# Two transformer blocks on one core: the first attention projects raw x in ten shared score steps

## The chip, the cores and the metric

The kernel runs on one core of a Trainium2 chip, in fp32, written in Bass with the Tile framework. The metric is the time of one execution on the device in microseconds (us). Lower is better. The engines of the core work beside each other: TensorE (PE, matmuls and transposes, with its weight loads PEld), VectorE (DVE), ScalarE (ACT), GpSimd (POOL) and SyncE (SP, which issues transfers). Line numbers such as L728 are lines of the kernel before.

## The reference

Two pre-norm blocks act on x of shape 8 x 512 x 256 (sequences, tokens, width):

```python
x = x + attention0(layernorm(x))   # 16 heads of 16, 4 k/v heads, rope, causal
x = x + moe0(layernorm(x))         # 32 experts, 8 per token, inner width 96
x = x + attention1(layernorm(x))   # 16 heads of 16, biases, causal
x = x + moe1(layernorm(x))         # 16 experts, 2 per token, inner 176, and a shared expert of 352

def attention0(x):                 # Wq 256x256, Wk and Wv 256x64, Wo 256x256
    q, k, v = rope(x @ Wq), rope(x @ Wk), x @ Wv
    att = softmax(where(causal, q k^T / sqrt(16), -inf))
    return (att @ v) @ Wo
def moe0(x):
    probs = softmax(x @ router_w.T)          # 32 logits per token
    rw, sel = top_k(probs, 8); rw = rw / sum(rw)
    return sum over chosen experts e of  rw_e * (silu(x @ wg_e) * (x @ wu_e)) @ wd_e
```

The layernorm has no scale and no shift: (x - mean) / sqrt(var + 1e-5), over the 256 features of a token.

## The kernel before

**Stages.** Attention 0 goes through the eight sequences. Beside sequence b it prepares sequence b+1 and finishes b-1: it adds the attention's output to x, normalizes, routes, and scatters each token's normalized row to 8 rows of a table in DRAM (`xg`), sorted by expert. Then the experts of layer 0 run tile by tile. Attention 1 gathers their results back to tokens, and has the same structure as attention 0. The experts of layer 1 come last.

**Score steps.** A sequence has four head groups c of four heads. Four blocks of keys j (128 keys each) are needed per group; block j meets only queries from 128j on, so it is 512, 384, 256 or 128 columns wide. `BANKS` makes three score steps of a group: block 0 (512 columns for each of four heads), blocks 1 and 3 together (512), block 2 (256). That is 12 steps per sequence. A step is: 4 or 8 matmuls into one tile `st` of four PSUM banks (L728; there is one such tile), one exponential on ACT from it to SBUF (L733; 2048 columns, or 1024 for block 2), and the causal mask by DVE on the diagonal squares (L739). The next step's scores can start when the exponential has read `st`. When a group's probabilities are masked, its 32 values products follow (L751), then a copy, four transposes to tokens (`turn`) and a division by the row sum.

**Order.** The order on PE is written by hand. `PLAN0` (attention 0) and `PLAN1` (attention 1) have one word per step; after the step's scores and exponential, each letter issues one piece of other work: c a values product, t its turn, m the mask, p a piece of `before` of the next sequence, q one of the sequence after that, a a piece of `finish` of the sequence before (output, then `after0`: normalization, routing, weights, tables), o the rest of the finish before that, g gathers. `planned` reads the words. DVE, ACT and POOL are ordered by the scheduler of the framework from priorities that follow the order of issue. `SENT` says how many of a sequence's 32 waiting scatters each step releases, 3, 3 and 2 in attention 0; a released scatter there is paced by that step's exponential.

**Preparing a sequence, attention 0** (`before`). x arrives transposed (`xf`, 256 features x 512 tokens). `load_x` turns it into tokens with 8 transposes and two ACT copies. DVE does statistics, the inverse root (L311 to L320) and the normalization (L358, 4 x 128x256). `turned` transposes the normalized x back (8 transposes L372, two ACT copies L373). Per tile of 128 tokens, two matmuls make q, k, v (384 columns, L952) and DVE does the rotations (three products L959 to L965, two sums) and a copy of v. Then q and k are transposed, with a copy each on ACT; k has two copies, each scaled by half[:,0:1] or half[:,1:2], one on ACT (L991) and one on DVE (L992).

**Finishing** (`finish`). `output` transposes the attention's output (two copies on ACT), makes two halves of the output product (8 matmuls of 256 columns each, L806) and adds each to x. `routed0` calls `layernorm` whole, in one piece of the order, then `turned`; `route` multiplies by the router (8 matmuls, L385), copies, transposes the logits (L393), and does maximum, difference, exponential (L405, ACT), the eight largest, weights, ranks within each expert (small matmuls L437, L439) and the list of scatters (L460).

## Time and profile before

| | us |
|---|---|
| median of the runs shown (1528.22, 1534.38, 1543.1) | 1534.38 |
| the profiled execution, its own time | 1529.75 |
| its span in the trace | 1528.0 |
| first exponential of attention 0 | 30.09 |
| first exponentials of its sequences 1 to 7 | 73.85, 115.80, 158.13, 201.01, 243.57, 288.90, 331.81 |
| experts 0, about | 380 to 805 |
| first exponentials of attention 1, sequences 0 to 7 | 808.28, 855.33, 906.23, 965.25, 1024.90, 1084.83, 1144.01, 1203.01 |
| experts 1, about | 1306 to 1490 |

The terms of the prediction are read from the trace as follows. The busy time of an engine is the sum of its instructions in a window. The timeline lists instructions of an engine in order: start, duration (with xN, of a run of N together), line, operation, output and inputs, partitions x columns; brackets give the idle time before the row and what ended it. The mean clock that TensorE was granted over this execution was 0.974 of full speed; where it is low, the same matmul takes longer.

### The profile page before, as it was taken

How to read it: one execution, taken by the hardware profiler on the slowest of the kernel's cores; microseconds unless marked ns; L12 is line 12 of the kernel's file. 1: busy time of each engine (PE TensorE's matmuls, PEld its weight loads, DVE VectorE, ACT ScalarE, POOL GpSimd, SP SyncE). 2: the span in 40 equal slices, each digit the busy share in tenths (PEclk: the TensorE clock that was granted, in tenths of full speed). 3: DMA queues.
4: the chain of work that ended last, by engine and by line, in shares of the span. 5: the costliest groups of instructions: out<-in, count | busy, mean ns of one | idle time of the engine just before them, and what ended most of it. 6: DMA issues, size and time to landing. Idle time of an engine off the chain costs nothing.

```text
span 1528.0 us, 29822 instructions
## 1 busy us (share of the span) xinstructions
PE 1405.0 (92%) x9856; PEld 960.7 (63%) x9856; DVE 949.3 (62%) x3121; ACT 666.6 (44%) x885; POOL 811.0 (53%) x674
## 2 busy tenths in 40 slices
PE   5889998887999899999998899999999988999994
PEld 3355555444889799999884445545455454777773
DVE  4678888776575566555565567677576564544454
ACT  2566666664233223333334455646645642122222
POOL 0004777777456100388878888888884203233433
PEclk8999999999999999999998999999999999999997
DMA  2023555336999786899997556566452005353346
GB/s 73 23 70 111 171 163 163 133 137 204 269 294 295 251 258 200 221 264 269 276 263 133 70 73 142 70 144 115 83 71 72 32 24 176 96 173 114 110 159 241
DMA packets 229312, 237.22 MB, mean 155 GB/s; under 512 B 77820, under 2 KB 209281, under 8 KB 229154
## 3 DMA queue, kind: packets, MB, share of 16 engines
q1 hardware_dynamic: 172930, 145.73, 32.3%
q0 software_dynamic: 55872, 89.18, 25.6%
q8 instruction: 84, 1.38, 0.4%
q14 instruction: 74, 0.61, 0.1%
q10 hardware_dynamic: 352, 0.33, 0.1%
HBM read 125.79 MB, written 110.92 MB: 155 GB/s over the span
## 4 chain that ended last, share of the span: by engine, by line
PE 59%; DVE 13%; POOL 8%; ACT 7%; issue 7%; DMA 5%; SPq 0%; DVEq 0%; ACTq 0%; POOLq 0%
PE gu_m L1314 16%; PE y_m L1343 11%; PE st_a L728 7%; PE o_a L751 5%; POOL x_a L1423 5%; ACT p_a L733 5%; PE xgT_m L1282 5%; POOL xg L460 3%; PE hT_m L1333 3%; DVE p_a L739 3%; DMA xg<-xn_f,rows_f 3%; PE sy_f L506 2%; PE sg_f L493 2%; PE k_a L1077 1%; PE su_f L493 1%
## 5 line engine op out<-in xcount | busy, mean ns | idle before, releaser
L460 POOL DMA_INDIRECT xg<-xn_f,rows_f x320 | 324.0, 1013 | 363.2 <-ACT p_a L733 134.7
L1423 POOL DMA_INDIRECT x_a<-yg,yrows x256 | 403.8, 1577 | 204.9 <-DMA xg_m<-xg 122.8
L733 ACT ACTIVATE p_a<-st_a 128x2048 f32<-128x2048 f32 (+1 forms) x192 | 306.1, 1594 | 233.4 <-PE st_a L728 132.4
L1314 PE MATMUL gu_m<-gw,xgTs_m 128*128 x1416 | 303.3, 358 | 0.4 <-DVE xgTs_m L1284 0.4
L1314 PEld LDWEIGHTS gu_m<-gw,xgTs_m 128*128 128x128 f32 x1416 | 235.2, 192 | 25.5 <-DVE xgTs_m L1284 1.2
L728 PE MATMUL st_a<-qT_a,kT_a 32*128 32x512 f32 (+3 forms) x2048 | 199.9, 483 | 34.6 <-ACT p_a L733 27.4
L1343 PE MATMUL y_m<-dw,hTs_m 96*128 (+1 forms) x860 | 216.9, 382 | 2.9 <-issue 2.9
L739 DVE TENSOR_TENSOR p_a<-p_a,causal 128x512 f32<-128x512 f32 x256 | 170.2, 683 | 76.1 <-ACT p_a L733 74.6
L1348 ACT COPY ys_m<-y_m 128x512 f32<-128x512 f32 x177 | 103.6, 585 | 175.1 <-PE y_m L1343 158.2
L1284 DVE COPY xgTs_m<-xgT_m 128x512 f32<-128x512 f32 x177 | 121.6, 687 | 85.4 <-PE xgT_m L1282 85.1
L728 PEld LDWEIGHTS st_a<-qT_a,kT_a 32*128 32x128 f32 x2048 | 88.4, 188 | 128.0 <-ACT p_a L733 55.1
L751 PE MATMUL o_a<-p_a,v 128*32 128x512 f32 (+3 forms) x2048 | 157.9, 447 | 10.3 <-DVE p_a L739 10.3
L1343 PEld LDWEIGHTS y_m<-dw,hTs_m 96*128 96x128 f32 (+1 forms) x860 | 150.1, 191 | 16.9 <-issue 3.1
L1306 DVE SCALAR_TENSOR_TENSOR h_m<-h_m,xg_m,gu_m 128x96 f32<-128x96 f32 (+1 forms) x354 | 104.0, 325 | 83.0 <-ACT h_m L1319 38.9
L1356 POOL DMA_INDIRECT yg<-ys_m,to_m x76 | 80.0, 1053 | 126.3 <-ACT ys_m L1348 113.5
L751 PEld LDWEIGHTS o_a<-p_a,v 128*32 128x32 f32 x2048 | 57.6, 111 | 130.5 <-issue 94.5
L1334 DVE COPY hTs_m<-hT_m 96x256 f32<-96x256 f32 (+1 forms) x177 | 83.9, 474 | 74.1 <-PE hT_m L1333 74.1
L1322 ACT ACTIVATE h_m<-gu_m 128x192 f32<-128x192 f32 x139 | 45.9, 330 | 176.7 <-PE gu_m L1314 162.7
L1282 PE MATMUL xgT_m<-ident,xg_m 128*128 128x128 f32 x708 | 110.4, 278 | 11.1 <-DMA xg_m<-xg 8.6
L1282 PEld LDWEIGHTS xgT_m<-ident,xg_m 128*128 128x128 f32 x708 | 88.2, 143 | 33.0 <-issue 13.0
L1333 PE MATMUL hT_m<-ident,h_m 128*96 128x128 f32 (+1 forms) x430 | 77.2, 275 | 0.3 <-DVE h_m L1306 0.2
L806 PE MATMUL y_a<-wo,oT_a 128*128 128x256 f32 x256 | 62.3, 388 | 5.0 <-DVE x_a L511 4.8
(249 smaller groups left out, 1614.5 us busy)
## 6 DMA issues: line engine op xcount, KB each, us to landing
xg_m<-xg SPq DMA_DIRECT2D x354, 144.0 KB
yg<-ys_m SPq DMA_DIRECT2D x139, 256.0 KB
g<-yg SPq DMA_DIRECT2D x16, 512.0 KB
xg<-zeros SPq DMA_DIRECT2D x50, 144.0 KB
xg<-xn_f,rows_f POOLq DMA_INDIRECT x320
x_after<-x_in SPq DMA_DIRECT2D x8, 512.0 KB
x_a<-x_after SPq DMA_DIRECT2D x8, 512.0 KB
x_a<-yg,yrows POOLq DMA_INDIRECT x256
```

What stands on the lines that cost most here:

```text
L460: inst = nc.gpsimd.indirect_dma_start(out=lay.xg, out_offset=bass.IndirectOffsetOnAxis(ap=rows[:, t, i : i + 1], axis=0), in_=xn[:, t, :], ...
L728: nc.tensor.matmul(st[:, g, at : at + T - j * P], kT[r, j * P : (j + 1) * P], qT[r, j * P :], start=True, stop=True,)
L733: self.newest = nc.scalar.activation(pt, st[:, :, :width], AF.Exp, scale=SCALE).ins
L739: self.masked = nc.vector.tensor_tensor(d, d, causal.unsqueeze(1).to_broadcast([P, NG, P]), ALU.mult).ins
L751: nc.tensor.matmul(o[32 * g : 32 * g + 32, j * P :], v1[:, j, v_at + g * (DH + 1) :][:, :32], probs[n][:, g, at : at + T - j * P], start=( ...
L1282: nc.tensor.transpose(tr[:, j, c, :], xg[:, j, c * P : (c + 1) * P], ident)
L1284: nc.vector.tensor_copy(xT, tr)
L1306: nc.vector.scalar_tensor_tensor(h[:, j, :], h[:, j, :], xg[:, j, D:][:, bass.ds(offs[part, i + j][2], 1)], gus[j][:, inner:], ALU.mult, A ...
L1314: nc.tensor.matmul(gus[j], xT[:, j, c, :], gu[:, bass.ds(at + c * 2 * inner, 2 * inner)], start=(c == 0), stop=(c == ND - 1),)
L1333: nc.tensor.transpose(hp[:n_in, q, j, :], h[:, j, lo : lo + n_in], ident)
L1343: nc.tensor.matmul(y[:, j, :], hT[:n_in, q, j, :], dn[:n_in, bass.ds(at + q * D, D)], start=(q == 0), stop=(q == n_ch - 1),)
L1423: inst = nc.gpsimd.indirect_dma_start(out=xs[b][:, t, :], out_offset=None, in_=lay.yg[: most_rows(b, again), :], in_offset=bass.IndirectOf ...
```

## The change

1. *Ten steps.* `STEPS` replaces `BANKS`. Two head groups form a pair with five steps: (group 0: block 0), (group 0: blocks 1, 3), (both groups: block 2, 256 columns each), (group 1: block 0), (group 1: blocks 1, 3). Each has an exponential of 2048 columns. This holds in both attentions. `ready` queues a group's values product when all its blocks have been through a step: after the third step of a pair for the first group, after the fifth for the second. The order strings are new, and `SENT` is 3, 3, 4, 3, 3.
2. *Raw x is projected* (attention 0). The weights of q, k, v and the router (32 more columns, 416 in all) are centred once: the mean of each column over the 256 features is made by a matmul with a matrix of 1/256 (`even`) and subtracted. So `xf` as it comes from DRAM is the input of the q, k, v matmuls, and neither the normalized x nor its transposition is needed; statistics and inverse root still are. The root is multiplied in by the rotations, now scalar_tensor_tensor, and by the copy of v. `xf` has two buffers. ACT copies the 32 router columns into `sums`.
3. *The router in the output product* (attention 0). Once, in sequence 1's preparation, `output_routing` makes Wo times the centred router weights, as 32 more columns of Wo. The output product is 288 wide, in four tiles of 128 tokens instead of two halves; DVE adds 256 columns to x and 32 to `sums`. So `sums` holds the logits of the new x, up to the root. `route` then has no router matmuls, copy or turn: it takes the maximum of `sums`, subtracts, multiplies by the root, ends its piece of the order, and takes the exponential in the next. The last sequence, routed beside the experts, goes the same way.
4. *Routed normalization in pieces.* `routed0` gives out statistics, root and normalization in pieces of the order of PE, not whole.
5. *Both copies of k* are on ACT. Three tiles (`q_in`, `turned0`, and the weights for `output_routing`) take room in other pools.

The diff, cut to its core:

```diff
-PLAN0 = "com optpm oapaom com apom atom acm qppm tqqm cm aappm tpm"
+PLAN0 = "ocmoo otom poaaom mc taapma comapa tpm qqqm cmpp taaam"
 TAIL0 = "otoaoaoaoa"
-PLAN1 = "cooggm oggm toggm coaggm aopggm taaoggm cppaoggm ppoggm taaopggm caopm aopam tapopm"
+PLAN1 = "cooggm ootggm oaggm coaggm toapggm acoggpm taaopggm ppaoggm caopggm taopppm"
 TAIL1 = "otaaoaaaoaoaoaa"
 PB = (3, 2)
-SENT = ((3, 3, 2), (1, 1, 1))
+SENT = ((3, 3, 4, 3, 3), (1, 1, 1, 1, 1))
...
-BANKS = [[0], [1, 3], [2]]
-QOFF = {0: (0, 0), 1: (1, 0), 3: (1, 3 * P), 2: (2, 0)}
+STEPS = [(0, [0]), (0, [1, 3]), (None, [2]), (1, [0]), (1, [1, 3])]
+QOFF = {0: 0, 1: 0, 3: 3 * P, 2: 2 * P}
...
+        roots[name] = rstd
         yield
+        if tag is None:
+            return rstd
...
+            if xT is None:
+                lg = sums.pop(b)
+            else:
...
+                nc.vector.tensor_tensor(pe, pe, roots.pop(name).unsqueeze(2).to_broadcast([P, NT, n_e]), ALU.mult)
+            if xT is None:
+                yield
             nc.scalar.activation(pe, pe, AF.Exp)
...
+        def blocks(self, at):
+
+            pair, n = divmod(at, len(STEPS))
+            side, js = STEPS[n]
+            return [(2 * pair + h, j, h if side is None else 0) for h in ((0, 1) if side is None else (side,)) for j in js]
+
+        def scores(self, b, at):
+
+            name = f"a{self.n}_{b}_{at}"
             st = self.ps.tile([P, NG, T], F32, tag="st", name=f"st_{name}", bufs=1)
-            for j in js:
-                at = QOFF[j][1]
+            pt = self.ptp.tile([P, NG, T], F32, tag="p2" if at % len(STEPS) == 2 else "p01", name=f"p_{name}", bufs=1 if at % len(STEPS) == 2 else PB[self.n])
+            for c, j, h in self.blocks(at):
...
+                self.probs[c, j] = pt, lo
+            self.newest = nc.scalar.activation(pt, st, AF.Exp, scale=SCALE).ins
...
+        def ready(self, at):
+
+            pair, n = divmod(at, len(STEPS))
+            done = 2 * pair + (n >= 2) + (n >= 4)
+            while self.next_c < done:
+                self.queue.append((self.b, self.next_c, self.probs))
+                self.next_c += 1
...
+            if self.n == 0:
+                for t in range(NT):
+                    y = self.bank(f"y_{name}_{t}")[:, : D + E0]
+                    for k in range(ND):
+                        nc.tensor.matmul(
+                            y, oT[:, k, t * P : (t + 1) * P], self.wo[:, k, :], start=(k == 0), stop=(k == ND - 1)
+                        )
+                    nc.vector.tensor_tensor(x[:, t, :], x[:, t, :], y[:, :D], ALU.add)
+                    nc.vector.tensor_tensor(sums[b][:, t, :], sums[b][:, t, :], y[:, D:], ALU.add)
+                    if t % 2:
+                        yield
+                return
...
+        nc.vector.tensor_copy(wq[:, :, width - E0 :], rw[:, 0, :, :E0])
+        even = awp.tile([P, P], F32, tag="even", name="even")
+        nc.vector.memset(even, 1.0 / D)
...
+        mean = bank("mean")[:, :width]
+        for k in range(ND):
+            nc.tensor.matmul(mean, even, wq[:, k, :], start=(k == 0), stop=(k == ND - 1))
+        for k in range(ND):
+            nc.vector.tensor_tensor(wq[:, k, :], wq[:, k, :], mean, ALU.subtract)
...
+                both = bank(f"wor_{k}")[:, :E0]
+                for m in range(ND):
+                    nc.tensor.matmul(
+                        both, woT[:, m, k * P : (k + 1) * P], wq[:, m, width - E0 :], start=(m == 0), stop=(m == ND - 1)
+                    )
+                nc.scalar.copy(wo[:, k, D:], both)
...
-            x = xs[b]
-            xn = layernorm(x, lnp, name)
+            xf = kept.pop(b)
+            root = whole(layernorm_steps(xs[b], lnp, name, None))
+            sums[b] = lasting[0].tile([P, NT, E0], F32, tag="sums", name=f"sums_{b}", bufs=3)
             yield
-            xn = yield from turned(xn, lnp, bank, name)
...
+                        tok[:, :width], xf[:, k, t * P : (t + 1) * P], wq[:, k, :],
...
+                nc.scalar.copy(sums[b][:, t, :], tok[:, width - E0 : width])
+                by = root[:, t : t + 1]
+                nc.vector.scalar_tensor_tensor(
+                    a, qk, by, cos[:, t, :].unsqueeze(1).to_broadcast([P, n_h, DH]), ALU.mult, ALU.mult
+                )
...
+                nc.vector.tensor_scalar(
+                    v_heads(v1, t, NG), tok[:, n_h * DH :][:, : HKV * DH].rearrange("p (g d) -> p g d", g=HKV),
+                    by, None, ALU.mult,
...
-            nc.vector.tensor_scalar(kT[:, 1, :], tr, half[:, 1:2], None, ALU.mult)
+            nc.scalar.activation(kT[:, 1, :], tr, AF.Copy, scale=half[:, 1:2])
...
-        xf = tmp.tile([P, ND, T], F32, tag="xf", name=f"xf{b}", bufs=1)
+        xf = tmp.tile([P, ND, T], F32, tag="xf", name=f"xf{b}", bufs=2)
...
-            xn = layernorm(xs[b], lnp, name, "xn_rows", 2, E0)
-            yield
-        xT = yield from turned(xn, lnp, bank, name)
-        yield from route(0, b, xn, xT, name, False)
+            xn = yield from layernorm_steps(xs[b], lnp, name, "xn_rows", 2, E0)
+        yield from route(0, b, xn, None, name, False)
```

## The prediction

> **What bounds the kernel now.** I read the page first. Its first part names TensorE (PE).
>
> ```profile
> PE 1405.0 (92%) x9856; PEld 960.7 (63%) x9856; DVE 949.3 (62%) x3121; ACT 666.6 (44%) x885; POOL 811.0 (53%) x674
> ```
>
> Then I cut the span into stages: the first attention 28 to 375 us (its sequences start where the first exponential of each starts), experts 395 to 805, the second attention 806 to 1256, the rest. One row each, of a steady sequence, the experts, and a steady sequence of the second attention (columns: window, its length, busy time of each engine, TensorE clock, DMA share, GB/s):
>
> ```profile
> core 0: us, PE busy (x) PEld busy (x) DVE busy (x) ACT busy (x) POOL busy (x), PEclk, DMA share, GB/s
> 201.01:243.57 42.56, 38.40 (x377) 21.99 (x376) 35.04 (x132) 27.35 (x29) 33.05 (x32) 1.00 0.56 173
> 395.00:805.00 410.00, 403.68 (x2520) 366.92 (x2519) 246.34 (x732) 131.75 (x284) 214.09 (x167) 0.99 0.95 262
> 1024.90:1084.83 59.93, 58.04 (x425) 31.09 (x421) 40.10 (x131) 33.71 (x32) 49.61 (x34) 1.00 0.62 103
> ```
>
> Experts and second attention are full (98 and 97%). The first attention is not: 4.2 us in 42.6 are gaps. Its timeline on PE shows three of them in the last quarter of a sequence; brackets give the idle time before a row and its releaser.
>
> ```profile
> 231.20 1.93 PE L751 MATMUL o_a<-p_a,v 128*32 128x512 f32 x24
> 235.06 0.64 PE L751 MATMUL o_a<-p_a,v 128*32 128x256 f32 x8 [1.93 <-DVE p_a L739]
> 235.63 1.15 PE L728 MATMUL st_a<-qT_a,kT_a 32*128 32x384 f32 x16
> 236.71 1.09 PE L372 MATMUL xT_f<-ident,xn_f 128*128 128x128 f32 x8
> 237.64 0.60 PE L982 MATMUL qT_a<-ident,qr_a 128*128 128x128 f32 x4
> 239.26 0.66 PE L982 MATMUL qT_a<-ident,qr_a 128*128 128x128 f32 x4 [1.02 <-ACT xT_f L373]
> ...
> 242.36 1.14 PE L728 MATMUL st_a<-qT_a,kT_a 32*128 32x512 f32 x8 [0.78 <-ACT kT_a L991]
> ```
>
> So PE work sets the pace, plus 3.7 us in which a mask comes late on a crowded VectorE (DVE) or a copy late on ScalarE (ACT). GpSimd (POOL) is as full, since each scatter is followed by 0.30 us:
>
> ```profile
> L460 POOL DMA_INDIRECT xg<-xn_f,rows_f x32 | 33.6, 1048 | 9.7 <-issue 8.8 <-ACT xT_f L373 0.3 <-ACT xT_a L373 0.3
> ```
>
> 33.6 + 8.8 = 42.4 of 42.56 us. In sequence 5 the tables of the first experts add a wait of PE on DVE, after which PE runs at half speed for some 3 us:
>
> ```profile
> 286.30 0.34 PE L1167 MATMUL ex<-past,step 32*1 32x106 f32 x2 [1.99 <-DVE past L1164]
> 286.48 0.34 PE L1169 MATMUL ro<-past,nt 32*1 32x106 f32 x2
> 286.75 2.09 PE L728 MATMUL st_a<-qT_a,kT_a 32*128 32x512 f32 x8
> 288.77 3.02 PE L751 MATMUL o_a<-p_a,v 128*32 128x512 f32 x32
> ```
>
> **The change, per sequence of the first attention.** Costs on PE are distances from start to start in the timeline at 201 to 243 us: scores of 512 columns 1.07, of 384+128 1.08, of 256 0.64, a values product 2.29, qkv of one tile 1.33 (384 columns), a half of the output 1.83 (8 matmuls of 256), four transposes 0.5.
>
> *Removed from PE*: transposes of the normalized x (1.0) and of the router's input (1.0), the router (0.55) and its turn (0.3): 2.85. *Added*: 32 columns on qkv and output. 0.229 us a matmul at 256 columns and 0.334 at 384 give 0.82 ns a column, so 16 matmuls take 16 x 32 x 0.82 ns = 0.4. PE work falls by 2.4.
>
> *ACT* loses four copies of 0.59 and one of 0.27, and gets four of 32 columns (0.19 each, on the line through 0.27 at 128 and 0.585 at 512) and the second k copy (0.69). That copy lies beside the 1.14 us of scores that the next exponential waits for; uncovered it costs 0.69. Ten exponentials of 1.88 replace eight of 1.88 and four of 1.03.
>
> *DVE* loses the normalization (1.37) and the k copy (0.74); it gains four adds of 32 columns (0.7), a multiply by the root (0.29) and smaller adds to x (4 x 0.42 for 2 x 0.68). The rotations become scalar_tensor_tensor. Row L1306 has such a one, 0.305 us at 96 columns, where the rotations' line (0.48 at 320, 0.311 at 160) gives 0.24; row L791 shows no surplus (0.217 at 64 columns). So 0 to 0.06 each, 0 to 0.7 for twelve; I take 0, the nearest plain form.
>
> *Ten steps.* A step is its scores and then other PE work until the exponential frees the score banks: 0.07 us to its start, 1.88, 0.06 back. So a step takes at least 3.15 us (3.3 with the two 256-column blocks). By the changed kernel's order on PE, steps 0 to 9 take 3.36, 3.16, 3.75, 3.36, 7.1 (a turn, four outputs, a qkv tile), 4.8, 3.15, 3.36, 4.4, 3.75 (the last holds its exponential and then 0.69 of k copy): 40.2.
>
> *The wait that is added.* On ACT the router's exponential stands ahead of the exponential of step 6. It needs DVE, and behind it on ACT wait a copy of sums and exponential 6, for which PE's step 7 waits. DVE has to do, after the fourth output: adds and statistics (1.6), a rotation (1.55 from start to start), more statistics, maximum and difference (0.85), the root's chain, two normalizations, one mask, two normalizations and the multiply. Rows of the chain:
>
> ```profile
> 223.28 0.35 DVE L311 TENSOR_SCALAR v_f<-mv_f 128x4 f32<-128x4 f32 x1
> ...
> 225.65 0.16 DVE L320 SCALAR_TENSOR_TENSOR rstd_f<-w_f,rstd_f 128x4 f32<-128x4 f32 x1
> 226.06 1.48 DVE L358 TENSOR_SCALAR xn_f<-x_in,mv_f,rstd_f 128x256 f32<-128x256 f32 x4 [0.25 <-DMA xg<-xn_f,rows_f]
> ```
>
> The chain is 2.15 from its second link (223.66) to 225.81, then 0.25 to the next row, 0.7 for two normalizations, 0.6 a mask, 0.7, and 0.3: 1.6 + 1.55 + 0.85 + 2.15 + 0.25 + 0.7 + 0.6 + 0.7 + 0.3 = 8.7. The fourth output ends at 19.4 of the sequence, so the input is there at 28.1; step 6's scores end at 26.7. Exponential 6 starts after the router's (0.3) at 28.45 in place of 26.8, and the sequence takes 40.2 + 1.7 = **41.9 us**. The masks for the third values product come after that on DVE and just fit.
>
> Sequences 1 to 6 took 257.96 us (the starts from 73.85 to 331.81), so 6 x 41.9 = 251.4 gains 6.5; I keep 0.5 for the tables, whose last matmuls now stand four steps behind their input: **-6.0**.
>
> *Start and end.* The first scores wait for rotation after rotation from 19.41 us on. Unnormalized, qkv can start when the weights are centred: last weight copy 9.2, mean matmuls 2.0 at the slow clock, two subtractions to 13.2, in place of 16.45; the root at 16.3 then holds the first rotation, and the last ends 3.6 earlier: **-3.6** (bounds -2 and -5). Sequence 0 (43.8 us): nine intervals of 3.3 to 5, and 9.3 for the three qkv tiles and rotations left to its end, 42.0: **-1.8**. Sequence 7 has no qkv work to cover the router's exponential (2.5 late), its last exponential is 0.85 longer and its output on the tail 0.4: **+3.0** with the shorter steps counted.
>
> *Elsewhere.* The last router's 1.9 us of PE work leaves the experts, where PE is full: **-1.9**. Second attention: its steps add up to 58.15 on PE, before 57.75 by the same sums; POOL has 32 gathers of 1.54 + 0.30 = 58.9 there, so **0** (bounds -5 and +8), and +0.8 for the longer last exponential. Second x buffer, the new places of three tiles, SENT: loads keep their order on SyncE and a scatter of sequence b must land 14 us before its rows are overwritten, cover enough; without it DVE waits as at 226.06. Ten paced groups still issue 32 scatters.
>
> Sum: -6.0 - 3.6 - 1.8 + 3.0 - 1.9 + 0.8 = -9.5, from the profiled execution's own 1529.75 (span 1528.0): **1520 us**. The median shown, 1534.38, lies 4.6 above that execution.
>
> **Rivals.** *DVE is not late*: then 40.2 a sequence, 6 x 1.7 + 2.5 = 12.7 more: 1507. For it: rows overlap on DVE more than I count; against: the same crowding cost 1.93 us at 235.06. *The gain is eaten*: with +0.06 on each rotation and the lateness doubled the sequences take 43.6, 7 x 1.7 = 12 back: 1532, so the change does nothing in the sum. *The clock drops*: PE ran its scores in 2.09 (1.14 elsewhere) and values in 3.02 (2.36) after stretches of 3.4 us with 1.43 and 1.55 us of PE work; after the 1.93 us idle at 235.06, with more work around it, scores still took 1.15. The change leaves 1.6 to 1.8 us of idle time in steps 6 and 9, so 1.6 to 1.8 of work. If both fall below some 1.6, two such slowings of 1.6 us in seven sequences cost 22: 1542, slower than before. [...]
>
> **Chances.** Forecast 0.45 (1513 to 1528), DVE not late 0.25, eaten 0.18, clock 0.12. Measurements of this kernel tell about 1% (15 us) from no change: runs lie between 1528 and 1543. Faster by over 1%: 0.25 and 0.05 of the forecast's edge, 0.30; slower: the clock and 0.02, 0.14; the rest 0.56. The range leaves out the outer halves of the first and last rivals: 1505 to 1537.
>
> **What would show it.** Starts of the first exponentials of sequences 1 to 6 some 41.9 us apart, first one near 26.5; an idle row of PE before the scores of step 7, released by ACT, which was itself released by DVE; PE busy near 36 in such a sequence; no half-speed scores near 280 us. Wrong if the second attention's 59 us moves by over 1 us, if rotations exceed 0.48, or if half-speed scores come in every sequence.

## The result

| | before | changed |
|---|---|---|
| median of 19 runs each, us | 1533.45 | 1526.64 |
| lowest to highest | 1527.94 to 1543.1 | 1520.57 to 1534.7 |
| ratio, with 95% interval | | 0.9959 (0.9944 to 0.9973) |
| profiled execution: span | 1528.0 | 1524.7 |

The change makes the kernel 0.4% faster, 6.8 us by the medians and 3.3 by the two profiled spans. A later comparison of the same two kernels gave 0.9939 (0.9916 to 0.9961). The forecast was 1520 with a range of 1505 to 1537. The time lies in the range and the sign is right, but 1520 lies 14 us below the median shown ahead of it (1534.38), over twice the gain that came, and the gain comes from another place. (The forecast's own sum is 9.5 us; it was taken from an execution 4.6 us below that median.) By the first exponentials of the sequences, as in the table of before:

| stage | forecast | measured | from |
|---|---|---|---|
| start, to the first exponential | -3.6 | +0.2 | 30.09 to 30.25 |
| sequence 0 of the first attention | -1.8 | +4.0 | 43.76 to 47.79 |
| its sequences 1 to 6 | -6.0 | -1.7 | 257.96 to 256.27 |
| its sequence 7, to the first expert matmul | +3.0 | +3.8 | 47.97 to 51.74 |
| experts 0, to the second attention's first exponential | -1.9 | -1.7 | 428.50 to 426.80 |
| second attention, first to last exponential | 0 | -9.5 | 442.99 to 433.48 |
| what follows | +0.8 | +1.6 | 276.73 to 278.37 |
| sum | -9.5 | -3.3 | |

So the first attention, the object of most of the change, loses 4.6 us with its experts, and the second, which I had put at nothing, gains 9.5.

The page of the changed kernel, its first part:

```profile
PE 1386.1 (91%) x9608; PEld 951.1 (62%) x9608; DVE 949.7 (62%) x3141; ACT 654.7 (43%) x857; POOL 812.7 (53%) x674
```

Its windows (columns as before): sequence 0, a steady sequence of the first attention, the experts, a steady sequence of the second attention.

```profile
30.25:78.04 47.79, 36.23 (x296) 18.81 (x300) 26.77 (x86) 26.24 (x29) 0.00 (x0) 0.82 0.04 12
205.97:248.06 42.09, 36.21 (x344) 19.74 (x340) 34.53 (x135) 26.02 (x27) 32.33 (x33) 1.00 0.56 175
395.00:805.00 410.00, 400.03 (x2496) 365.95 (x2495) 246.45 (x736) 130.19 (x281) 206.56 (x160) 0.99 0.94 260
969.81:1027.65 57.84, 56.97 (x421) 31.86 (x417) 40.08 (x129) 33.50 (x29) 47.68 (x34) 1.00 0.61 119
```

TensorE (PE) did lose 2.2 us of work in the steady sequence of the first attention (38.40 to 36.21), and the sequence only 0.5 (42.56 to 42.09). Where the rest went stands on PE's timeline:

```profile
230.03 1.15 PE L745 MATMUL st_a<-qT_a,kT_a 32*128 32x384 f32 x16
...
231.60 1.56 PE L1016 MATMUL qkv_a<-wqkv,xf 128*128 128x416 f32 x4
234.75 1.15 PE L745 MATMUL st_a<-qT_a,kT_a 32*128 32x256 f32 x16 [1.58 <-ACT p_a L750]
235.82 0.66 PE L1554 MATMUL xin<-ident,xf 128*128 128x128 f32 x4
238.01 0.63 PE L1554 MATMUL xin<-ident,xf 128*128 128x128 f32 x4 [1.53 <-DVE otok_a L784]
```

and on ScalarE's (ACT):

```profile
232.53 0.31 ACT L415 ACTIVATE ev_f<-ev_f 128x128 f32<-128x128 f32 x1 [3.32 <-DVE ev_f L412]
232.75 0.17 ACT L1023 COPY sums<-qkv_a 128x32 f32<-128x32 f32 x1
232.81 1.88 ACT L750 ACTIVATE p_a<-st_a 128x2048 f32<-128x2048 f32 x1
```

The scores of step 6 are done at 231.18, but its exponential starts at 232.81, behind the router's, which waited 3.32 us for VectorE (DVE). Step 7 on PE waits 1.58 for it. This is the wait that the prediction put into each sequence, at its place and in its size.

The chip matters for all that follows. On three of the five chips of the experiments the kernel before, too, took 1657 to 1671 us (medians), and sequences of 42 us took 46 to 62 (last section). I call these chips disturbed. On them I use the ratios (time over that of the kernel before on the same chip, with a 95% interval), and sequences 0 and 1, which take there what they take elsewhere.

### The profile page after: what moved, and what is told of

Same layout as the page of the kernel before. It is cut to its first block, busy times and chain, and to the rows that moved or that the text cites. A ratio compares the mean times of both kernels' runs of the same rounds, so it can differ in the third digit from the quotient of the medians.

```text
span 1524.7 us, 29311 instructions
## 1 busy us (share of the span) xinstructions
PE 1386.1 (91%) x9608; PEld 951.1 (62%) x9608; DVE 949.7 (62%) x3141; ACT 654.7 (43%) x857; POOL 812.7 (53%) x674
## 4 chain that ended last, share of the span: by engine, by line
PE 58%; POOL 11%; issue 5%; DMA 4%; DVE 3%; ACT 3%; SPq 0%; DVEq 0%; ACTq 0%; POOLq 0%
PE gu_m L1385 18%; PE y_m L1414 12%; POOL x_a L1494 10%; PE xgT_m L1353 5%; PE st_a L745 4%; PE o_a L768 3%; PE hT_m L1404 3%; ACT p_a L750 2%; PE sg_f L503 2%; PE sy_f L516 2%; PE su_f L503 2%; PE y_a L842 1%; PE v_a L1129 1%; DMA xg<-xn_f,rows_f 1%; DMA xg_m<-xg 1%
## 5 line engine op out<-in xcount | busy, mean ns | idle before, releaser
L750 ACT ACTIVATE p_a<-st_a 128x2048 f32<-128x2048 f32 x160 | 300.4, 1877 | 187.0 <-PE st_a L745 85.3
L745 PE MATMUL st_a<-qT_a,kT_a 32*128 32x512 f32 (+3 forms) x2048 | 192.7, 480 | 58.8 <-ACT p_a L750 49.2
L745 PEld LDWEIGHTS st_a<-qT_a,kT_a 32*128 32x128 f32 x2048 | 92.2, 190 | 133.5 <-ACT p_a L750 72.8
L768 PEld LDWEIGHTS o_a<-p_a,v 128*32 128x32 f32 x2048 | 57.7, 112 | 122.0 <-issue 92.0
L1404 PEld LDWEIGHTS hT_m<-ident,h_m 128*96 128x96 f32 (+1 forms) x430 | 52.8, 125 | 16.7 <-issue 6.4
```

Of the source, the lines that this page charges most:

```text
L745: nc.tensor.matmul(st[:, g, lo : lo + T - j * P], kT[r, j * P : (j + 1) * P], qT[r, j * P :], start=True, stop=True,)
L750: self.newest = nc.scalar.activation(pt, st, AF.Exp, scale=SCALE).ins
L768: nc.tensor.matmul(o[32 * g : 32 * g + 32, j * P :], v1[:, j, v_at + g * (DH + 1) :][:, :32], pt[:, g, lo : lo + T - j * P], start=(step = ...
L1404: nc.tensor.transpose(hp[:n_in, q, j, :], h[:, j, lo : lo + n_in], ident)
```

## The experiments

**1. Which attention gains: one changed, the other as before.** Attention 1 alone:

```diff
-BANKS = [[0], [1, 3], [2]]                 # both attentions
+STEPS = (twelve steps, ten steps)          # first, second
-PLAN1 = "cooggm oggm toggm ... tapopm"
+PLAN1 = "cooggm ootggm oaggm ... taopppm"
```

> The kernel before with the second attention alone changed: ten steps, its new order, its scatters one per step. The first attention is the old one (twelve steps, normalized x, router by its own matmuls). Theory: the whole gain of the changed kernel is made in the second attention (its eight sequences 9.5 us shorter from first to last exponential in the two traces, the stretch behind it 1.6 longer), so this kernel gains 8 us over the kernel before: span 1520, ratio to before 0.995, faster than the changed kernel by 3 to 5 us, and steady sequences of the second attention at 57.7 us. Rival: the second attention runs shorter because the changed first attention and experts leave the gathers at another time; then its sequences stay at 59 to 60 us and the span at 1527 to 1529.

And attention 0 alone, the changed kernel with the twelve steps and the old order in the second:

> The changed kernel with the second attention as before (twelve steps, old order). Theory: the changed first attention loses 4.6 us up to the first exponential of the second (812.85 against 808.28), so this kernel is slower than the kernel before: span 1532 to 1533, ratio 1.003, steady sequences of the second attention back at 59 to 60 us. Rival (the second attention gains through the first): span 1525, ratio 0.996, sequences at 57.7.

Measured, on one chip: the second alone 0.9934 (0.9891 to 0.9977), the first alone 1.0053 (1.0014 to 1.0093). The gain is the second attention's, and the first by itself makes the kernel slower. The second alone once more, on another chip:

> Ten steps in the second attention with the new order, all else as in the kernel before, once more: steady sequences 57.6 to 57.9 us as in the changed kernel (the gain does not need the changed first attention), span 1519 to 1522, ratio 0.994, and 3 to 5 us below the run with the old order.

0.9887 (0.9851 to 0.9923), and 0.5% below the ten steps with the old order on that chip (0.9939, 0.99 to 0.9978, experiment 5; the two intervals overlap). Both chips were disturbed ones, so neither spans nor steady sequences can be held against the expectations; what the ratios show is that the gain is there without the changed first attention. On the undisturbed chips the new second attention was measured only behind the changed first one, with steady sequences of 57.6 to 57.9 us in every profile.

**2. The wait for the router's exponential, and sequence 0.** First each edit alone:

```diff
+            with tc.issue_after(exponential of step 6 of the sequence):
                 nc.scalar.activation(pe, pe, AF.Exp)
```

> The changed kernel with the router's exponential put behind the seventh score exponential on ScalarE instead of ahead of it, in sequences 1 to 7. Theory of the prediction (the late input of the router's exponential holds the score exponential, and TensorE's eighth step behind it): the idle 1.2 to 1.6 us ahead of the eighth step's scores go in sequences 1 to 4, 2.0 in sequence 6 and 4.1 in sequence 7, 8 to 10 us in all; span 1515 to 1517. Rival: VectorE sets the pace of the second half of a sequence, so that what goes there comes back as a wait for a mask, a rotation or a division one or two steps on: span 1522 to 1526 with sequences 2 and 4 still near 42 us.

```diff
 PLAN0 = "ocmoo otom poaaom mc taapma comapa tpm qqqm cmpp taaam"
+PLAN00 = "ppm pom ppm mcp tppm cmp tpm qqqm cmpp tm"     # sequence 0
```

> The changed kernel with an order of its own for sequence 0, in which the pieces that prepare sequence 1 stand in all ten steps (two in each of the first three), instead of six pieces in the steps and six behind the last one. Theory: sequence 0's 47.8 us are steps 0 to 3 at half clock, since TensorE has little beside the scores (17.4 us for about 13 at full clock), and 11.7 us of preparation uncovered behind its last scores. With the pieces moved, the clock rises earlier and the uncovered part falls to 4 to 6 us: sequence 0 takes 39 to 42 us, and the span falls by 6 to 9 to 1516 to 1519. Rival: the clock of the first 15 us of scores does not depend on what stands between them, and the rotations, not the order, set the end of the sequence: 45 to 47 us, span 1522 to 1525.

Ratios 0.9947 (0.9911 to 0.9984) and 0.9934 (0.9894 to 0.9974), on a disturbed chip where the changed kernel itself was not run; sequence 0 fell to 44.3 us with its own order. Then both in one kernel, beside the changed kernel on a chip like the first:

> The changed kernel itself, beside the runs that follow, on their chip. The chip of the four runs before this one was slower by 130 us with the kernel before too, all of it from the sequences on in which scatters and gathers run. Expected if this chip is like the first: ratio to before 0.996, span 1523 to 1526, sequences of the first attention 47.8, 43.6, 41.8, 42.5, 42.1, 44.4, 41.9 us.

> Both edits of the two runs before in one kernel: the router's exponential behind the seventh score exponential (it acts from the second sequence on) and the own order of sequence 0 (it acts there alone), so each shows in its own sequences. Theory: sequence 0 takes 41 to 44.5 in place of 47.8 us (it took 44.3 on the slower chip, where it was undisturbed), sequences 2 and 4 take 40.3 to 41 in place of 41.8 and 42.1, and sequence 7 loses its 4.1 us wait: 4 + 6 x 1.3 + 3 = 15 us, span 1510 against the changed kernel's 1524.7, ratio to before 0.988. Rival (VectorE sets the pace of a sequence's second half): sequences 2 and 4 within 0.5 us of 42, and only the 4 us of sequence 0 are gained: span 1520.

The changed kernel: 0.9939, span 1526.4, sequences 47.78, 43.62, 42.13, 42.51, 42.10, 43.39, 40.11. Both edits: **0.9873 (0.9842 to 0.9905)**, span 1512.6, faster than both kernels. Its sequences take 42.71, 41.37, 41.48, 42.08, 41.97, 43.61, 41.41, and from the last sequence's first exponential to its last 33.2 in place of 38.1 (36.5 in the first profile of the changed kernel). The span lies between theory and rival, nearer the theory. Against the changed kernel on the same chip sequence 0 gains 5.1, sequence 1 2.2, sequences 6 and 7 together 3.6; but the steady sequences 2, 3 and 4 gain 0.6, 0.4 and 0.1, as the rival said. Their timeline on PE has no wait ahead of step 7 any more, and a new one in the values products two steps on:

```profile
228.47 1.14 PE L747 MATMUL st_a<-qT_a,kT_a 32*128 32x512 f32 x8 [0.36 <-ACT p_a L752]
229.54 1.93 PE L771 MATMUL o_a<-p_a,v 128*32 128x512 f32 x24
233.52 0.64 PE L771 MATMUL o_a<-p_a,v 128*32 128x256 f32 x8 [2.05 <-DVE p_a L759]
```

In the stretch that ends there DVE is full (window, columns as before):

```profile
214.00:233.50 19.50, 16.68 (x136) 8.12 (x134) 18.83 (x81) 9.71 (x11) 14.93 (x16) 1.00 0.79 224
```

18.83 of 19.50 us. The mask that PE waits for stands on DVE behind 2.5 us of the router's eight largest, weights and ranks, which followed its exponential to the later place. Whether the mask put ahead of them on DVE would end the wait was not tried.

**3. Is it VectorE, and which part of its work?** The root left out, in the changed kernel and then in the kernel with both edits:

```diff
-nc.vector.scalar_tensor_tensor(a, qk, by, cos_t, ALU.mult, ALU.mult)   # and twice sin, and v
+nc.vector.tensor_tensor(a, qk, cos_t, ALU.mult)
```

> The changed kernel without the root in the rotations and in the copy of v (plain products and a plain copy; the normalization of q, k and v is left out, all else stays). In the trace of the changed kernel the rotation's products take 0.55, 0.37, 0.37 us and the copy of v 0.27, where they took 0.48, 0.31, 0.31 and 0.21: 0.25 us a tile, 1.0 us a sequence on VectorE. Theory: at the start four rotations stand on the path, so the first exponential comes 0.8 to 1.0 us earlier (29.3); in a sequence only the part ahead of the router's exponential counts (one rotation, 0.25 us), as long as that exponential is what TensorE waits for: span 3 us shorter, 1521 to 1522. Rival (VectorE is the bound of these sequences): 1 us a sequence, 8 us in all, 1516.

0.9948 (0.9924 to 0.9973), span 1522.3; the first exponential came at 28.98 (1.3 earlier), sequences 2 and 4 took 41.72 and 41.66 (0.4 less than the changed kernel on that chip, 0.1 and 0.4 less than its first profile). So, near the theory's 0.25, a steady sequence gains a part of the 1.0 us and not the whole: while the router's exponential holds TensorE, only the rotation ahead of it counts. Sequence 6 took 47.07 (41.87 and 40.11 in the two profiles of the changed kernel) and ate 5 us of this. The router's input comes late from DVE there in the changed kernel too, where the exponential stands behind the score exponential of step 7 and waits 2.6 us for it; here the scheduler put it one place earlier, behind that of step 6, where it waited 4.8 us and held step 8 by 6.0. The next kernel has the same in its sequence 6 (45.35). One step in ACT's order is worth that much.

> The kernel with both edits (exponential behind, own order of sequence 0), and the root left out of the rotations and of v besides (the normalization of q, k and v is left out): 1.0 us less on VectorE in each sequence, nothing else. With both edits the steady sequences 2 and 4 took 41.5 and 42.0 us, where 40.3 to 41 was expected, and TensorE waits 2.05 us for a mask in the ninth step. VectorE as the bound: these sequences fall by 0.8 to 1.0 us, to 40.5 to 41.1, and the span by 6 or 7. GpSimd as the bound (32 scatters of 0.96 + 0.30 and some longer make 41 to 42 us): no change in sequences 2 to 5, and only the start and sequences 0 and 1 gain, 2 us in all.

0.9879 (0.9837 to 0.9922), span 1507.4 in spite of sequence 6; sequences 2 to 5 took 40.99, 41.43, 41.05, 42.68, each 0.5 to 0.9 less than with both edits alone, and sequence 1 0.7 less. (On this chip the kernel of experiment 4 with both edits and an earlier start has 41.48, 42.11, 41.99 and 43.63, the same difference.) The wait for the mask shrank from 3.8 to 2.2 us in two sequences. With GpSimd (POOL) as the bound nothing would have moved.

```diff
-nc.scalar.activation(kT[:, 1, :], tr, AF.Copy, scale=half[:, 1:2])
+nc.vector.tensor_scalar(kT[:, 1, :], tr, half[:, 1:2], None, ALU.mult)
```

> The kernel with both edits, and the second copy of k back on VectorE, as in the kernel before: 0.74 us more on VectorE in each sequence and 0.69 less on ScalarE. The counterpart of the run before. VectorE as the bound: sequences 1 to 6 take 0.5 to 0.75 us more, span 3 to 5 us longer. GpSimd as the bound, or ScalarE: no change, or 0.1 us less where the first exponential of a sequence stands behind the second copy.

0.9899 (0.9863 to 0.9934), span 1515.3. Sequences 1 to 4 took 41.37, 41.49, 42.10 and 42.01, to 0.04 what they took without: 0.74 us more on DVE cost nothing there. Half of my theory falls with it: the bound is not DVE's work over a sequence but what it has to do between the fourth output and the masks of step 7; the k copy lies behind that. The 2.7 us of span are from the start (first exponential 31.30 in place of 30.48) and from sequences 5 and 6 (1.8 together). Fewer scatters, which would price GpSimd, were not tried, since expert tiles would then hold undefined rows.

**4. The clock in sequence 0.** Earlier start, by making the mean of the weights behind the cosines:

> The kernel with both edits, and the matmuls that make the mean of the weights put behind the transposes of the cosines instead of ahead of them. In the changed kernel the cosines' transposes wait behind the mean (12.95 us), the buffer that the sines are loaded into comes free behind them, the sines land at 15.4 and their transposes stand ahead of the first projection (15.76), for which the weights are ready at 14.6. Theory: the projection starts at 14.6 to 14.9 and the first exponential comes 0.7 to 1.4 us earlier (29.0 to 29.7), held then by the root (17.57) and the rotations; span 1 us shorter than with both edits, 1511 to 1512. Rival: the rotations on VectorE alone set it: 30.2 to 30.5, no change.

0.9906 (0.9871 to 0.994), span 1512.3. The first exponential came at 28.99, 1.5 earlier, and sequence 0 took 44.31 in place of 42.71: at the second sequence's start (73.30 against 73.19) all of it was gone. In both kernels PE ran its first values product at half speed (4.18 and 4.05 us, where the changed kernel's at 49.75 took 2.36) and was at full speed from about 46 us on. So I read it that sequence 0 ends here by when the clock rises. It is one pair of executions, though: the own order alone took 44.27 from a start at 30.37, and the kernel of experiment 3 with both edits and without the root, which started at 28.21, kept that (42.83, second sequence at 71.04): its clock rose earlier, within the first values product (2.91 us, done at 44.4). The changed kernel's timeline on PE there (its granted clock was 0.50 from 30.25 to 42.40, 0.71 from there to 45.50 and 0.95 from there to the second sequence):

```profile
32.18 2.09 PE L745 MATMUL st_a<-qT_a,kT_a 32*128 32x384 f32 x16 [2.00 <-ACT p_a L750]
36.27 2.09 PE L745 MATMUL st_a<-qT_a,kT_a 32*128 32x256 f32 x16 [2.00 <-ACT p_a L750]
38.29 1.11 PE L1554 MATMUL xin<-ident,xf 128*128 128x128 f32 x4
40.36 2.09 PE L745 MATMUL st_a<-qT_a,kT_a 32*128 32x512 f32 x8 [0.95 <-ACT p_a L750]
42.38 3.22 PE L768 MATMUL o_a<-p_a,v 128*32 128x512 f32 x32
45.53 1.15 PE L745 MATMUL st_a<-qT_a,kT_a 32*128 32x384 f32 x16
```

```diff
+                if att.n == 0 and b == 0 and at in (0, 1, 2):
+                    for i in range(8):
+                        nc.tensor.transpose(filler[...], ident, ident)
```

> The changed kernel with eight idle transposes behind the scores in steps 0 to 2 of sequence 0 (1.0 us at full clock, 2.0 at half), whose result nobody reads; nothing waits for them but TensorE itself. In two profiles of the changed kernel scores 1 to 3 run at half speed (2.09 us) until 42.4, with 2.0 us of idle time ahead of each, and TensorE gets fast behind some 4 us of unbroken work; in the kernel before that came at 36 us, behind the eight transposes of x in step 1. Theory (gaps in TensorE's work keep the clock down): with the gaps filled scores run in 1.15 from 32 to 36 us on and sequence 0 takes 43 to 45 in place of 47.8, and the sequences behind it are as before. Rival (the time of the clock's rise has nothing to do with the work): 47 to 48.

0.9896 (0.9832 to 0.996). With the gaps filled by work that nobody reads, PE is fast ten us earlier:

```profile
31.13 1.73 PE L745 MATMUL st_a<-qT_a,kT_a 32*128 32x384 f32 x16
32.79 1.10 PE L885 MATMUL fill<-ident 128*128 128x128 f32 x8
34.87 1.15 PE L745 MATMUL st_a<-qT_a,kT_a 32*128 32x256 f32 x16 [0.98 <-ACT p_a L750]
```

Sequence 0 took 45.31 in place of 47.8, 0.3 more than was expected.

> The kernel with both edits, and eight idle transposes behind the scores of steps 1 and 2 of sequence 0, where TensorE sat idle for 2.0 us and fell back to half speed (scores 2.09 and values 3.9 us in place of 1.14 and 2.3). Theory: sequence 0 takes 39 to 41 in place of 42.7, the span falls to 1509 to 1511, ratio 0.985. Rival: 42.5 to 43, span 1512 to 1513, or longer where the clock falls later instead.

Sequence 0 took 40.86, as expected; ratio 0.9879 (0.9822 to 0.9937), on a disturbed chip. With the earlier start as well:

> The changed kernel with the router's exponential behind, the own order of sequence 0, the mean of the weights behind the cosines, and eight idle transposes in steps 1 and 2 of sequence 0. Sequence 0 took 40.9 with the filled gaps and 44.3 where the earlier start was eaten by a clock that rose no earlier. Theory (the clock follows the work): first exponential at 29.0 to 29.7, sequence 0 in 40 to 42, the second sequence starts at 69.5 to 71.5 in place of 73.2, span 1509 to 1511, ratio 0.985. Rival: the clock eats the start again, 73, span 1512.

First exponential 29.17, sequence 0 40.86, the second sequence starts at 70.03: with the gaps filled the earlier start is kept. Ratio 0.9868 (0.9827 to 0.9908), again on a disturbed chip, where the second attention alone had 0.9887; on that ground I don't call it better than both edits.

**5. What gains in the second attention.** PE's waits over sequences 3 and 4 (window 965.25 to 1084.83) in the kernel before: total, times, longest.

```profile
PE y_a L806 <- DVE x_a L511: 2.3, 2, 1.1
PE sg_f L493 <- ACT hs_f L497: 0.7, 2, 0.4
PE xT_f L372 <- DVE v L1063: 0.6, 2, 0.3
```

The same in the changed kernel (969.81 to 1085.34):

```profile
PE st_a L745 <- ACT p_a L750: 1.5, 2, 0.8
```

So of the 1.8 us that sequence 3 lost (59.65 to 57.84), 1.0 is idle time (1.88 to 0.87: 59.65 - 57.77 and 57.84 - 56.97) and 0.8 is work; of the 2.2 us of sequence 4 (59.93 to 57.69), 1.0 and 1.2. One letter first:

```diff
-PLAN1 = "... taaoggm cppaoggm ..."
+PLAN1 = "... taoggm acppaoggm ..."
```

> The kernel before with one letter of the second attention's order moved: the second half of the output product goes from the end of the sixth step to the head of the seventh step's work, so that it no longer stands right behind the first half. Twelve steps stay. Theory: of the 1.9 us by which a steady sequence of the second attention became shorter (59.65 to 57.75), the wait of that second half for a bank that VectorE frees late makes 1.1, and two score steps fewer the rest (0.5 of 256-column blocks that share a step, 0.3 of changes between kinds of matmul): sequences 58.3 to 58.8 us here, span 1522 to 1524. Rival: the gain is the ten steps' alone, and the wait moves to another row: 59 to 59.9 us, span 1527 to 1529.

The sequences took 59.13, 59.47, 59.76 and 59.17, against 59.02, 59.65, 59.93 and 59.18: the rival. The wait of 1.1 was gone and stood two steps on, as 1.2 us ahead of the transposes of the routed x, for DVE as well. (Ratio 0.9978, 0.996 to 0.9996.)

```diff
+PLAN1 = "cooggm ootggm oaggm coaggm toaggm pm acoggpm taaopggm ppaogm caopggm taopgpm pm"   # twelve steps
```

> The kernel before, with the changed kernel's order of the second attention stretched over the old twelve score steps (each shared step is taken apart into two, the letters of the work between stay in their sequence); scores, exponentials and blocks are as before. Since the moved letter of the run before only moved the wait, two readings of the 1.9 us a sequence are left. Order: the new order has no waits of TensorE on VectorE (1.0 us of the 1.9 by the two traces, idle 1.9 down to 0.9), and 0.9 is TensorE work that goes with the two score steps: then the steady sequences take 58.4 to 58.8 us here and the span falls by 4 to 6, ratio 0.997. Ten steps alone: the new order without them changes nothing, sequences 59.2 to 59.9 us, ratio 1.000.

1.0189 (1.0153 to 1.0225), sequences of 63 to 66 us: neither reading. PE waited 2.5 us for DVE ahead of the same transposes, which then took 1.54 us in place of 0.60. The new order, stretched so, is bad.

```diff
+PLAN1 = "cooggm oggm toggm coaggm aoptaaoggggm cppaoggm ppoggm taaopggm caopm aopatapopm"   # ten steps
```

> The kernel before with ten score steps in the second attention, in the old order: the letters of each step stay where they were, those of the sixth and twelfth step go behind those of the fifth and eleventh, whose steps now come last of their pair. The new order over twelve steps had cost 5.5 us a sequence, so order and steps hang together. If the ten steps alone make the gain: steady sequences 57.6 to 58.4 us, span 1519 to 1522. If the order is needed as well: the waits of TensorE on VectorE stay (1.8 us a sequence in the kernel before) and only TensorE's 0.9 us less work shows, 58.5 to 59.2 us, span 1523 to 1526; a sequence longer than 59.7 would say that the old order suits ten steps worse than twelve.

> Ten steps in the second attention with the old order, all else as in the kernel before, once more. From the one undisturbed sequence of the run before: ten steps take 0.75 us a sequence, and the wait of the second half of the output product for VectorE (1.5 to 1.8 us) stays. So steady sequences of 58.2 to 58.9 us, span 1523 to 1526, ratio 0.997. Against it: 57.6 to 57.9, then the order gives nothing, span 1519 to 1521; 59.2 and more, then the steps give nothing.

0.997 (0.9917 to 1.0022) and 0.9939 (0.99 to 0.9978), both on disturbed chips. The first run's seventh sequence lies behind the gathers: 58.24 us, against 59.00 before and 57.65 changed. Its largest wait:

```profile
PE y_a L822 <- DVE x_a L511: 1.5, 1, 1.5
```

So the ten steps give some 0.75 us a sequence with the old order, whose wait stays, and the new order some 0.6 on top. It is one sequence on one chip (three rows of "issue" with 1.1 us stand in it, where records of matmuls are missing), so the split is a reading and not more; that steps and order hang together is shown by the twelve steps in the new order.

## Why the prediction was right or wrong

That the time lies inside the range is luck. By the table of stages the start and the eight sequences of the first attention came out 14.7 us worse than forecast and the second attention 9.5 better, so that most of the errors cancel. Two of the three signs of being wrong that the prediction named came: the second attention's sequences moved by 1.8 to 2.2 us, and the rotations took 0.55.

- **The second attention, "0 (bounds -5 and +8)", is the step that failed most.** It rested on two readings. "Its steps add up to 58.15 on PE, before 57.75": the windows have 57.77 before and 56.97 after in sequence 3, so PE's work fell by 0.8 (1.2 in sequence 4) where my sum let it rise by 0.4. The blocks of 256 columns take 2.9 us in the old steps and 2.3 in the shared ones by the groups, and two steps fewer are two changes between kinds of matmul fewer (the q and k products, 1.72 each from start to start among themselves, take 1.8 to 1.95 ahead of scores). I had taken start-to-start distances of matmuls that stood ahead of scores and used them for the new places too. "POOL has 32 gathers of 1.54 + 0.30 = 58.9 there": true, and no bound. The last gather started at 1154.26 in place of 1146.94, while the sequences ran at 57.7; they are issued ahead, so PE ran away from them. And I did not look for waits to go: 1.0 us a sequence. How the gain divides between the ten steps and the new order stays open (experiment 5).
- **Steady sequences, 41.9: right.** Sequences 2 and 4 took 41.83 and 42.09 (3 took 42.50), with the wait at its place (1.58 for 1.7). This was not luck: from scores to scores the steps of sequence 4 took 3.36, 3.15, 3.54, 3.36, 6.94, 4.96, 4.72 with the wait, 3.82, 4.51 and 3.73, each within 0.5 of the sum's. A wait of 1.53 for a division on DVE in step 7 was not in it; shorter steps ahead of it made up for that. The rival "DVE is not late" (40.2) was not only not the case: experiment 2 took the router's exponential away, and DVE was late two steps on. That the price would move rather than go was nowhere in my text; and with 1 us of DVE's work taken away besides, sequences 2 to 4 still took 41.0 to 41.4 and not the 40.2 of PE's steps.
- **Rotations "0 to 0.06 each... I take 0": the wrong end.** They took 0.55, 0.37 and 0.37 (0.48, 0.31, 0.31 before), v 0.27 (0.21): the surplus that row L1306 had shown. It costs 0.1 to 0.4 us a steady sequence as the order stands and 0.5 to 0.9 once the exponential is moved.
- **Start -3.6: failed.** The forecast had the weights centred at 13.2 and the projection behind that. The mean's matmuls took 3.14 and not 2.0; and the cosines' transposes wait behind them, the sines' load behind these for its buffer, and the sines' transposes stand ahead of the projection on PE, for a load of their own:

```profile
12.95 0.60 PE L969 MATMUL cost<-ident,cosf 16*128 16x16 f32 x4
15.43 0.39 PE L969 MATMUL sint<-ident,sinf 16*128 16x16 f32 x4 [1.88 <-DMA sinf<-in_a_dram]
15.76 7.55 PE L1016 MATMUL qkv_a<-wqkv,xf 128*128 128x416 f32 x16
```

  The root came at 17.57 for 16.3, the rotations took 1.77 a tile for 1.53. I had followed the moved step's matmuls and not its place in the queue; the place in the queue cost 1.5 (experiment 4), the root in the rotations 1.3 (experiment 3).
- **Sequence 0, -1.8: failed, by the clock and by the uncovered end.** The prediction had the clock as a rival in the steady sequences (0.12), where it stayed at 1.00, and none at the start: steps 0 to 3 took 17.4 us, with scores at 2.09. And from the last scores to the first of sequence 1 it had 9.3 us, where it took 11.7:

```profile
64.18 1.15 PE L745 MATMUL st_a<-qT_a,kT_a 32*128 32x384 f32 x16
...
73.76 0.76 PE L1053 MATMUL qT_a<-ident,qr_a 128*128 128x128 f32 x5 [1.44 <-DVE qr_a L1036]
...
75.84 2.09 PE L745 MATMUL st_a<-qT_a,kT_a 32*128 32x512 f32 x8 [0.88 <-ACT kT_a L1062]
```

  The filled gaps took 2.5 us off sequence 0 (experiment 4), the own order, which spreads that end over the steps, 3.5 to 5.1 (experiment 2). Seven profiles of the old first attention take 43.76 to 47.83 us in sequence 0, four of them 43.8, and four of the new one 47.63 to 48.02; so the change costs up to 4 us there. In the profile of before the scores are at 1.14 us from 38.49 on, in that of the changed kernel at 2.09 until 42.4; that this makes the difference in the other profiles too is my reading.
- **Sequences 1 to 6, -6.0, were -1.7** though the steady ones were right: sequence 1 starts at half speed (scores 2.09, values 4.24; +1.7), and the tables of sequence 5 still hold PE 1.86 us and the clock behind it (44.38; "no half-speed scores near 280 us" is refuted at 290.23).
- **Sequence 7 (+3.0; +3.8), the experts (-1.9; -1.7) and the k copy (covered) were right.** The uncovered router's exponential makes a wait of 4.13 there (2.5 in the forecast), and scores at 1.39 and 2.09 behind it.

## To carry to other kernels

Here work taken off the full engine was a gain only as far as the next queue allowed (2.2 us off TensorE in a steady sequence gave 0.5): price the change with the removed wait and with the next engine's queue in that stretch (VectorE, with both edits 97% busy over the 19.5 us before a mask, 82% over a sequence of the changed kernel). A stage that was "97% full" still gained: 1.0 us a sequence of idle time, where waits of 0.3 to 1.1 us had stood, and 0.8 to 1.2 us of TensorE's work; look at a stage's waits before putting it at nothing. And the gaps of 2.0 us in sequence 0 were dear on TensorE: idle transposes in them bought 2.5 us in the changed kernel (47.8 to 45.31) and 1.9 with both edits (42.71 to 40.86).

## What was not expected of the hardware

*The clock.* In sequences 1 to 7 of the first attention of the changed kernel's profile, nine gaps of 1.35 to 1.58 us ahead of scores left these at 1.14 and 1.15 us, while gaps of 1.86, 2.00, 4.13 and 1.98 were followed by scores at 2.09, 1.39, 1.39 and 2.09 (granted clock 1.00 from 286.00 to 289.80, 0.59 from 290.23 to 294.00):

```profile
289.84 0.46 PE L1240 MATMUL ro<-past,nt 32*1 32x106 f32 x2 [1.86 <-DVE otok_a L784]
290.23 2.09 PE L745 MATMUL st_a<-qT_a,kT_a 32*128 32x512 f32 x8
...
323.29 1.39 PE L745 MATMUL st_a<-qT_a,kT_a 32*128 32x512 f32 x8 [2.00 <-ACT p_a L750]
324.61 3.75 PE L768 MATMUL o_a<-p_a,v 128*32 128x512 f32 x32
```

The same 2.00 us gap in the changed kernel's second profile was followed by scores at 1.14, and sequence 6 took 40.11 in place of 41.87 (sequence 7 then took 1.6 longer). Others (before at 355.79, both edits at 282.18 and 233.52) cost nothing either; a third with both edits, at 314.05, left the scores at 1.14 and ran the values behind them at half speed (4.05). Equal gaps cost in one place and not in another, and one start 1.5 us earlier left the rise at the same time (experiment 4). What sets the rise and the fall is not shown by these runs.

*Chips.* On three chips the kernel before took 1657 to 1671 us, some 130 more than on the others, and the traces there (of variants of both kernels) are longer beside scatters and gathers. The same scatters took 1.01 to 1.03 us there and 1.01 to 1.02 elsewhere, but engines stood still for what the profile calls "remote" or "issue". In the kernel with the router's exponential put behind, on ACT and then on PE:

```profile
253.19 0.59 ACT L775 COPY osb_a<-o_a 128x512 f32<-128x512 f32 x1 [8.05 <-remote]
```

```profile
282.20 0.40 PE L746 MATMUL st_a<-qT_a,kT_a 32*128 32x128 f32 x2 [0.97 <-issue]
283.63 0.38 PE L746 MATMUL st_a<-qT_a,kT_a 32*128 32x128 f32 x2 [1.04 <-issue]
285.05 0.38 PE L746 MATMUL st_a<-qT_a,kT_a 32*128 32x128 f32 x2 [1.04 <-issue]
```

PE goes on two matmuls at a time here, with 0.97 to 1.04 us of idle time before each pair; no run was made to show why.
